# A GRU with expert-choice routing: w_ih by columns on two queues, six pairs of steps multiplied in the head, block products a quad further ahead, and an expert pair's sums in two PSUM banks

## The chip, the cores and the metric

The kernel runs on one core of one Trainium2 chip. The metric is the device time of one execution in microseconds. The program has five engines with queues of their own: TensorE (PE in the profile, with its weight loads as PEld), VectorE (DVE), ScalarE (ACT), GpSimd (POOL) and SyncE (SP, which only issues transfers here). All data is float32, apart from zeros for clearing sums and the counts of the bit search.

## The reference, cut to what matters

```python
gi = x @ W_ih + b_ih;  gh = h @ W_hh + b_hh         # x: 16 x 256 x 512, h: 16 x 512
r = sigmoid(i_r + h_r);  z = sigmoid(i_z + h_z)
n = tanh(i_n + r * h_n)
h = (1 - z) * n + z * h                             # 256 steps, one after the other
S = softmax(states @ router_w + router_b)           # 4096 tokens x 16 experts
G, idx = top_k(S.T, 256)                            # each expert takes its 256 best tokens
out = x + scatter_add(idx, G * (states[idx] @ expert_w + expert_b))
```

All experts share one matrix `expert_w` (512 x 512), so a token's output is its input plus the sum of its gates (G of the experts that took it) times one product of its state. The kernel computes that product for all tokens and multiplies by the gate at the end.

## The kernel before

**Head (lines 430 to 765).** The weights w_ih (3 MB, four row blocks k of 768 KB) and w_hh (3 MB, three gates of 1 MB) and the first two groups of x are loaded on the queues of SP and ScalarE. A group is 8 steps of 16 rows. A pair is two steps. The x-part of the gates (x @ W_ih) of the first four pairs is computed directly: `x_part` (L608) adds one row block k of one pair into a PSUM bank out of the list `held`, k by k as the blocks arrive, and `x_done` (L623) copies the bank with the bias into `ring`, which holds the x-parts of AHEAD = 6 pairs. Meanwhile `mixes` (L635) subtracts column blocks of w_ih from each other on VectorE, for the fast block products of the loop. `keep_clock` fills TensorE's idle time with matmuls of zeros.

**Loop (from L777).** One step s multiplies the state `hs` by w_hh (`h_part`, recorded at L700: 48 matmuls of 32 columns of the array, 96 records), first for r and n, then for z. While ScalarE and VectorE then compute r, tanh, the transposes and the new hs, TensorE is given other work of about the same length, the fill of a step:

- `x_product` (L656, records at L673): the x-parts of later steps, a quad (four steps, two pairs) at a time. A quad's 2 x 2 block product is made of seven block products instead of eight, spread over four steps, with sums kept in `x_bank0`, `x_bank1` and part of `l_bank`. `quad = s // 4 + 2` is the one under work.
- the router's logits of finished groups (in steps marked `apart`), and products of finished states by `expert_w` for the groups 0 to 9 (`expert`, L581), with a bank of `ps_m` per group. `expert_done` copies a finished half out.
- in the last two steps the first pair products of the tail (`expert_for`).

The order on the engines is written out by hand: within `manual_schedule` every engine takes its instructions in the order of the text. VectorE's side work of a step stands after its chain: `x_sums` and `turn_x` (transposing x for the next groups, loaded as `xa` by SP eight steps ahead), `less_max` (maximum for the softmax), `make` (sums of state blocks for pair products) and `mix` (differences of blocks of `expert_w`). They are bound to the position c of a step in its group of eight.

**Tail.** The groups 10 to 27 are taken as nine pairs. For a pair `expert_product` (L284, records at L304) makes seven block products with five sums a to e, each half a PSUM bank wide; ScalarE presets a and e with the bias (`preset_a` L186, `preset_e` L189), copies b from a, c from b, d from b (`copy_of`, L193), and drains finished sums (`drain`, L203 for e, L208); VectorE adds e to the sums of the right halves (L217, or L212 straight from the bank once the gate is known). The order of a pair is

```python
for n, of in ((1, i + 1), (3, i), (7, i), (5, i + 1), (4, i), (2, i + 1), (6, i + 1)):
    yield from expert_product(n, of)
```

so the products of two pairs alternate, and each copy has another pair's product beside it. A yield is half a product's k; `expert_for(n)` runs n units, where a unit is four matmuls of 128 columns. The last four groups are multiplied directly (`late_part`, L111, records at L115). Three banks serve a pair:

```python
pool_of = [(ps_m, "pe"), (ps_m, "pe"), (ps_x, "x0"), (ps_x, "x1"), None, None]
which, half = {"a": (0, lo), "d": (0, hi), "b": (1, lo), "c": (2, lo), "e": (2, hi)}[name]
```

The two entries None are banks of `ps_e`, a pool that is opened only after the loop; until then `catch_up`, which does the copies of finished products, stops at those that need it.

Between the last step and the gate lie the softmax, the transposes of the probabilities and `by_bits` (L1008): a search of 15 bits for each expert's 256th largest probability, one count over all tokens per bit, with seven units of pair products beside each bit. After the gate (L1126, made at L1050) the remaining units run in a loop over `parts`. A counter `owed` rises by 9 with each part, and at 20 a finished group is multiplied by the gate, added to x (`add_gated`, L1056) and stored. At part CHECK = 48 the threshold is counted once more.

Of the kernel before, what the change touches and what calls it, by code (L numbers as in the profile page):

```python
# [17 lines left out]
def kernel(  # L18
# [18 lines left out]
    P = 128  # L37
# [90 lines left out]
    pairs = [(g, g + 1) for g in range(N_EARLY, NG - 4, 2)]  # L128
    pool_of = [(ps_m, "pe"), (ps_m, "pe"), (ps_x, "x0"), (ps_x, "x1"), None, None]
    gated = []  # L130

    def new_bank(i, which):
        pool, tag = pool_of[3 * (i % 2) + which]
        return pool.tile([P, D], F32, name="pe" if tag == "pe" else tag, tag=tag)

# [9 lines left out]
    made += [set_of(room[:, 8 * HD + 4 * HD * i :]) for i in range(N_SETS)]  # L145
    parted = [room[:, 8 * HD + 4 * HD * N_SETS + HD * i :][:, 0:HD] for i in range(2)]
    eb_d = room[:, 10 * HD + 4 * HD * N_SETS :][:, 0:HD]

# [32 lines left out]
    def region(i, name):  # L181
        which, half = {"a": (0, lo), "d": (0, hi), "b": (1, lo), "c": (2, lo), "e": (2, hi)}[name]
        return bank_of(i, which)[:, half]
# [52 lines left out]
    def end_of(i):  # L236
        drain(i, "db")
        if i + 2 < len(pairs):
            preset_a(i + 2)
            preset_e(i + 2)  # L240
        else:
            first = 3 * (i + 2 - len(pairs))
            later.extend((i, n, item) for n, item in enumerate(last_items[first : first + 3]))
            preset_last()

    later = []

    def preset_last():
        i, n, (g, cols) = later.pop(0)
        pe = new_bank(i, n)  # L250
        nc.scalar.copy(pe[:, cols], eb[:, cols])
        last_sums[g, cols.start] = pe
# [23 lines left out]
    def catch_up():  # L276
        while todo:
            n, i = todo[0]
            if pool_of[3 * (i % 2) + 1] is None and n in (1, 5, 6, 7):
                break  # L280
            del todo[0]
            after(n, i)
# [49 lines left out]
    def late_parts():  # L332
# [15 lines left out]
        for item in range(1, len(last_items)):  # L348
            if later:
                preset_last()  # L350
            yield from last_product(item)
# [9 lines left out]
    with (  # L361
# [77 lines left out]
        with tc.manual_schedule(engines={ET.SP, ET.Activation, ET.Pool}):  # L439
            def load_gate(gate, queue, ks=slice(0, KC)):  # L440
                queue.dma_start(
                    out=whh[:, ks, gate, :],
                    in_=w_hh[:, gate * D : (gate + 1) * D].rearrange("(c p) n -> p c n", c=KC)[:, ks, :],
                )

            def load_k(k, queue):
                queue.dma_start(
                    out=wih[:, k].rearrange("p g d -> p (g d)"),
                    in_=w_ih.rearrange("(p c) n -> p c n", c=KC)[:, k, :],
                )  # L450

            nc.gpsimd.dma_start(out=c0, in_=cond)
            nc.sync.dma_start(out=xs[:, 0, :], in_=x[:, 0:TG, :])
            load_k(0, nc.scalar)
            load_k(1, nc.scalar)
            load_k(2, nc.sync)
            load_k(3, nc.sync)
            load_gate(0, nc.scalar)
            nc.sync.dma_start(out=xs[:, 1, :], in_=x[:, TG : 2 * TG, :])
            load_gate(2, nc.sync)  # L460
            load_gate(1, nc.scalar, slice(0, KC - 1))
            load_gate(1, nc.sync, slice(KC - 1, KC))
            nc.scalar.activation(dummy, ones[0:1, 0:1], AF.Sigmoid)
            for dst, src in (
                (b_raw[0:1], b_ih.rearrange("(o g d) -> o g d", o=1, d=D)),
                (b_raw[1:2], b_hh.rearrange("(o g d) -> o g d", o=1, d=D)),
                (b_n, b_hh[2 * D :].rearrange("(o d) -> o d", o=1)),
            ):
                nc.gpsimd.dma_start(out=dst, in_=src)
# [164 lines left out]

        def mixes(part):  # L635
# [4 lines left out]
            nc.vector.tensor_tensor(dst, one, other, ALU.subtract)  # L640

# [75 lines left out]
        with tc.manual_schedule(engines={ET.PE, ET.Activation, ET.DVE, ET.Pool}):  # L717
# [3 lines left out]
            keep_clock(8)  # L721
            held = (r_bank, n_bank, z_bank, x_bank0, x_bank1)

# [12 lines left out]
            for k in range(KC):  # L736
                for p in range(KC):
                    x_part(p, k, held[p], start=False)
                if k == 1:
                    mixes(0)  # L740
                elif k == 2:
                    mixes(1)
                    mixes(3)
                elif k == 3:
                    mixes(2)
                if k == 1:
                    for c in range(KC):
                        nc.tensor.transpose(
                            idles[1][:, B * c : B * (c + 1)], c0[:, P * c : P * (c + 1)], ident[0:B, 0:B]
                        )  # L750
                    nc.vector.tensor_copy(
                        hs[:, :, 0, :], idles[1][:, 0 : KC * B].rearrange("p (k b) -> p k b", b=B)
                    )
                elif k == 2:
                    biases(l_bank)
                    nc.vector.tensor_copy(bias, l_bank.rearrange("p (g d) -> p g d", d=P))
                    nc.scalar.copy(a_sum, bias_f[:, 0:C2])
                    nc.vector.tensor_tensor(spare, bias_f[:, C2 : 2 * C2], bias_f[:, 0:C2], ALU.subtract)
            for p in range(KC):
                x_done(p, held[p])  # L760
                if p == 0:
                    preset_first(0)
                elif p == 2:
                    preset_rest(0)
            spread_x(1, idles[0])
            keep_clock(HEAD_FILL)

        first, second = range(KC // 2), range(KC // 2, KC)

        with tc.manual_schedule(engines={ET.PE, ET.Activation, ET.DVE, ET.Pool, ET.SP}):  # L770
# [6 lines left out]
            for s in range(T):  # L777
# [5 lines left out]
                h_part(s, "z", range(KC))  # L783
                q4, quad = s % 4, s // 4 + 2

# [8 lines left out]

                late_four = q4 == 0 and 2 < quad <= NQ
                if late_four:
# [28 lines left out]
                if s == T - 1:  # L825
                    logits(lgt, range(KC), range(NG - 1, NG), slice(0, TG - 1))
                if s >= T - 2:
                    expert_for((6, 2)[s - T + 2])

# [84 lines left out]
                if apart and c == 6:  # L914
                    less_max(g // KC - 1, lgt)
                if done and s > 6 * TG and (c in (1, 2, 4) or quad >= NQ):
                    g_, half = done.pop(0)
                    expert_done(g_, half)
                    copied += half
                elif s > (N_EARLY + 11) * TG and while_x and c in (1, 2, 4):  # L920
                    make(*while_x.pop(0))

                if c == 0 and g < NG - 1:
                    x_sums(g + 1)
                elif c in (5, 6) and g + 2 < NG:
                    turn_x(g + 2, xa_next, slice(2 * (c - 5), 2 * (c - 4)))

                if c >= KC:
                    if 5 < g < N_EARLY:
                        load_x(g, c - KC, s)  # L930
                elif g + 2 < NG:
                    if c == 0:
                        xa_next = new_xa()
                    nc.gpsimd.tensor_copy(xa_next[quadrant(c), 0, 0:1], hs[quadrant(c), 0, slot(s), 0:1])
                    load_xa(g + 2, xa_next, c, (nc.sync, nc.sync))
                if s > T - TG:
# [46 lines left out]
    with (  # L983
# [5 lines left out]
    ):  # L989
        pool_of[4] = pool_of[5] = (ps_e, "pe")  # L990
# [4 lines left out]
        parted += [rt.tile([P, HD], F32, name=f"part{i}") for i in range(len(pairs) - 2)]  # L995
        by_row = lambda ap: ap.rearrange("p (q b t) -> p b q t", q=QG, b=B)
# [77 lines left out]
        with tc.manual_schedule(engines={ET.PE, ET.Activation, ET.DVE}):  # L1074
# [5 lines left out]
            ps_last = ps_n.tile([P, P], F32, name="ps_last", tag="n")  # L1080
            preset_e(1)
            lg_f = lg.rearrange("p e g -> p (e g)")
# [44 lines left out]

            gated += [add_gated, send]
            owed = 20
# [115 lines left out]
```

## Time and profile before

| | us |
|---|---|
| median of 3 runs | 1117.0 |
| lowest and highest | 1116.86, 1117.44 |
| the profiled execution | 1116.54 |
| its span, first to last instruction | 1114.5 |
| TensorE busy | 1103.0 (99%) |
| VectorE busy | 800.8 (72%) |
| ScalarE busy | 578.7 (52%) |
| gates of step 0 start | 21.00 |
| gates of step 1 start | 26.43 |
| pair products after the gate start | 1073.90 |
| last matmul ends | 1109.56 |

The span is the time from the first instruction to the last; the time of an execution has some 2 us more around it. The profile gives each engine's busy time in the span. A chain of waits follows back from the last instruction what released it; groups of instructions are named by line, engine and tile, with the number of records behind an x. A matmul in float32 leaves two records.

### The profile page before, as it was taken

The page shows a single profiled execution, that of the slowest core. Times are in us where ns is not written, and L with a number is a line of the kernel's source. Part 1 is how long each engine was busy: PE and PEld are TensorE (multiplying, and loading weights), DVE is VectorE, ACT ScalarE, POOL GpSimd, SP SyncE. Part 2 cuts the span into 40 slices and gives each one's busy share as a digit, 9 for nine tenths or more (in the row PEclk, how much of TensorE's full clock was granted, in tenths as well). Part 3 has the DMA queues.
Part 4 walks back from the last instruction along what each step waited for, and adds up shares of the span by engine and source line. Part 5 has one row for each costly group of instructions (what it writes and reads, how often), then busy time and mean ns, then how long its engine had stood idle before and what let it go on. Part 6 is the DMA issues. An engine that isn't in the chain of part 4 may idle for free.

```text
span 1114.5 us, 77084 instructions
## 1 busy us (share of the span) xinstructions
PE 1103.0 (99%) x34242; PEld 956.1 (86%) x34242; DVE 800.8 (72%) x4663; ACT 578.7 (52%) x2648; POOL 31.0 (3%) x176
## 2 busy tenths in 40 slices
PE   8999999999999999999999999999999999999998
PEld 4888888888888888888888888888888888888663
DVE  5666676776767777766767777777777777767885
ACT  1455555555555555555555555555555555554541
POOL 1000000000000000000000000000000000000000
PEclk9999999999999999999999999999999999999999
DMA  7200000000000000000000000000000000003346
GB/s 251 61 13 14 14 14 14 11 21 21 21 21 16 14 14 12 11 12 12 14 14 14 14 12 11 12 12 14 15 14 14 13 12 12 10 5 99 112 144 205
DMA packets 34370, 37.33 MB, mean 33 GB/s; under 512 B 6112, under 2 KB 23776, under 8 KB 34032
## 3 DMA queue, kind: packets, MB, share of 16 engines
q1 hardware_dynamic: 32688, 28.90, 9.0%
q8 instruction: 269, 4.41, 1.7%
q10 hardware_dynamic: 1216, 3.41, 0.9%
q14 instruction: 69, 0.57, 0.2%
q0 software_dynamic: 128, 0.05, 0.0%
HBM read 23.94 MB, written 8.39 MB: 29 GB/s over the span
## 4 chain that ended last, share of the span: by engine, by line
PE 92%; DVE 4%; DMA 2%; ACT 1%; issue 1%; SPq 0%; ACTq 0%; DVEq 0%
PE gates L700 59%; PE x L673 21%; PE gates L673 4%; PE pe L581 3%; PE pe L304 3%; DMA whh<-in_L_cond_W_hh_dram 2%; PE x L304 1%; PE pe L115 1%; DVE nT L882 1%; DVE t L844 1%; DVE zT L885 1%; ACT r L787 1%; ACT t L848 1%; DVE v L893 0%; PE x L115 0%
## 5 line engine op out<-in xcount | busy, mean ns | idle before, releaser
L700 PE MATMUL gates<-whh,hs 128*16 128x128 f32 x24576 | 722.7, 273 | 4.1 <-DVE hs L896 2.3
L700 PEld LDWEIGHTS gates<-whh,hs 128*16 128x16 f32 x24576 | 652.0, 103 | 59.1 <-DVE hs L896 51.5
L787 ACT ACTIVATE r<-gates 128x128 f32<-128x128 f32 x256 | 71.1, 278 | 231.2 <-PE gates L700 231.2
L791 DVE COPY seen<-r 1x1 f32<-1x1 f32 x256 | 36.0, 141 | 201.4 <-ACT r L787 201.3
L885 DVE STREAM_TRANSPOSE zT<-zs 128x32 f32<-128x32 f32 (+1 forms) x768 | 165.8, 216 | 0.7 <-ACT zs L850 0.7
L848 ACT ACTIVATE t<-t 128x64 f32<-128x64 f32 x512 | 103.1, 248 | 103.7 <-DVE t L846 103.7
L882 DVE STREAM_TRANSPOSE nT<-t 128x64 f32<-128x64 f32 x512 | 100.3, 234 | 48.0 <-ACT t L848 48.0
L893 DVE TENSOR_TENSOR v<-u,zT 128x32 f32<-128x32 f32 x512 | 98.7, 193 | 8.8
L673 PE MATMUL x<-wih,xt 128*32 128x192 f32 (+1 forms) x2000 | 103.6, 325 | 0.0
L896 DVE TENSOR_TENSOR hs<-v,nT 128x32 f32<-128x32 f32 x512 | 95.5, 187 | 8.7
L673 PE MATMUL x<-wih,xs 128*32 128x192 f32 x1984 | 92.0, 326 | 0.0
L846 DVE TENSOR_TENSOR t<-t,xs 128x64 f32<-128x64 f32 x512 | 90.7, 219 | 0.0
L844 DVE TENSOR_TENSOR t<-r,gates 128x64 f32<-128x64 f32 x512 | 90.1, 217 | 0.0
L850 ACT ACTIVATE zs<-gates 128x64 f32<-128x64 f32 x512 | 86.8, 221 | 0.8 <-PE gates L700 0.8
L888 DVE TENSOR_TENSOR u<-hs,nT 128x32 f32<-128x32 f32 x512 | 78.4, 153 | 0.0
L673 PEld LDWEIGHTS x<-wih,xt 128*32 128x32 f32 x2000 | 63.6, 110 | 12.0
L673 PEld LDWEIGHTS x<-wih,xs 128*32 128x32 f32 x1984 | 63.2, 110 | 12.1
L506 ACT COPY ht<-hs 128x128 f32<-128x128 f32 (+1 forms) x128 | 51.9, 407 | 0.7 <-DVE hs L896 0.7
L673 PE MATMUL x<-xs 128*32 128x192 f32 (+1 forms) x1056 | 51.7, 316 | 0.0
L673 PE MATMUL x<-xs,xt 128*32 128x192 f32 x992 | 51.7, 326 | 0.0
L673 PE MATMUL gates<-xs 128*32 128x192 f32 x992 | 51.7, 326 | 0.0
L866 ACT COPY x<-x 128x192 f32<-128x192 f32 x62 | 18.8, 303 | 63.0 <-PE x L673 63.0
(200 smaller groups left out, 931.6 us busy)
## 6 DMA issues: line engine op xcount, KB each, us to landing
out_dram<-xs SPq DMA_DIRECT2D x31, 256.0 KB, 3.0
xa<-in_x_dram SPq DMA_DIRECT2D x240, 32.0 KB, 3.0
xs<-in_x_dram SPq DMA_DIRECT2D x28, 256.0 KB, 4.0
wih<-in_L_cond_W_ih_dram ACTq DMA_DIRECT2D x2, 768.0 KB, 6.9
wih<-in_L_cond_W_ih_dram SPq DMA_DIRECT2D x2, 768.0 KB, 10.6
whh<-in_L_cond_W_hh_dram ACTq DMA_DIRECT2D x1, 1024.0 KB, 16.6
whh<-in_L_cond_W_hh_dram SPq DMA_DIRECT2D x1, 1024.0 KB, 18.6
ewr<-in_L_ffn_expert_w_dram SPq DMA_DIRECT2D x4, 256.0 KB, 3.2
```

What stands on the lines that cost most here:

```text
L673: nc.tensor.matmul(dst[quadrant(j), at:to], lhs[:, QD * k : QD * (k + 1)], columns(rows[k], j)[:, at // QD : to // QD], start=False, stop= ...
L700: nc.tensor.matmul(dst[quadrant(j, m)], lhs, columns(whh[:, k, gate_, :], j), start=False, stop=(k == KC - 1), tile_position=(0, QD * j), ...
L787: nc.scalar.activation(r, rr[p % 2], AF.Sigmoid)
L844: nc.vector.tensor_tensor(t[half], r[:, cols], hn[p % 2][:, cols], ALU.mult)
L846: nc.vector.tensor_tensor(t[half], t[half], ring[:, p % AHEAD, 2, cols], ALU.add)
L848: nc.scalar.activation(t[half], t[half], AF.Tanh)
L850: nc.scalar.activation(zs[half], zz[p % 2][:, cols], AF.Sigmoid)
L882: nc.vector.transpose(nT[half], t[half])
L885: nc.vector.transpose(zT[half][:, part], zs[half][:, part])
L888: nc.vector.tensor_tensor(u[half], hs[:, halves[half][2], slot(s), :], of_step(nT[half], odd), ALU.subtract)
L893: nc.vector.tensor_tensor(v[half], u[half], of_step(zT[half], odd), ALU.mult)
L896: nc.vector.tensor_tensor(hs[:, halves[half][2], slot(s + 1), :], v[half], of_step(nT[half], odd), ALU.add)
```

## The change

1. **Head.** Each row block of w_ih is split by columns over the two queues (1024 and 512 columns of the 1536, or 768 and 768). Each gate of w_hh is split in halves by row blocks, in the order r, n, z. The third group's x (`xa`) is loaded in the head. Six pairs instead of four are multiplied directly: four as before, then the second group's x is transposed, and after the row blocks the pairs 4 and 5 follow. The fourth `mixes` goes in halves to steps 0 and 1.
2. **Loop.** The quad under work is `s // 4 + 3`, so the block products end four steps earlier. `x_sums`, `turn_x` and the loads of `xa` move by four steps and one group, and `expert_done` and `make` go to other positions c. The last steps get six units per step for the early groups, and from step 249 on pair products of the tail. `mix` begins at step 244, `preset_a` and `preset_e` at step 248.
3. **Two banks.** A pair's five sums take two banks: a and d share a half, one after the other, e has the other half; b and c share the second bank. The two banks of `ps_e` go to the last groups.
4. **Stores.** `owed` rises by 11 per part, and CHECK is 36.

```diff
-    pool_of = [(ps_m, "pe"), (ps_m, "pe"), (ps_x, "x0"), (ps_x, "x1"), None, None]
+    pool_of = [(ps_x, "x0"), (ps_x, "x1"), (ps_m, "pe"), (ps_m, "pe")]
...
-        which, half = {"a": (0, lo), "d": (0, hi), "b": (1, lo), "c": (2, lo), "e": (2, hi)}[name]
+        which, half = {"a": (0, lo), "d": (0, lo), "e": (0, hi), "b": (1, lo), "c": (1, hi)}[name]
...
-            if pool_of[3 * (i % 2) + 1] is None and n in (1, 5, 6, 7):
-                break
...
-            load_k(0, nc.scalar)
-            load_k(1, nc.scalar)
-            load_k(2, nc.sync)
-            load_k(3, nc.sync)
-            load_gate(0, nc.scalar)
-            nc.sync.dma_start(out=xs[:, 1, :], in_=x[:, TG : 2 * TG, :])
-            load_gate(2, nc.sync)
-            load_gate(1, nc.scalar, slice(0, KC - 1))
-            load_gate(1, nc.sync, slice(KC - 1, KC))
+            for k, at in enumerate((third_k, half_k, half_k, third_k)):
+                load_k(k, nc.scalar, slice(0, at))
+                if k == KC - 1:
+                    nc.sync.dma_start(out=xs[:, 1, :], in_=x[:, TG : 2 * TG, :])
+                load_k(k, nc.sync, slice(at, 3 * D))
+            for gate in (0, 2, 1):
+                for queue, ks in ((nc.scalar, slice(0, KC // 2)), (nc.sync, slice(KC // 2, KC))):
+                    load_gate(gate, queue, ks)
+            xa_next = new_xa()
+            for c in range(KC):
+                load_xa(2, xa_next, c, (nc.sync, nc.sync))
...
-            held = (r_bank, n_bank, z_bank, x_bank0, x_bank1)
+            held = (r_bank, n_bank, z_bank, x_bank0, x_bank1, idles[1])
...
-                elif k == 2:
-                    mixes(1)
-                    mixes(3)
-                elif k == 3:
-                    mixes(2)
...
+                    spread_x(1, idles[0])
+                    x_sums(1)
+                elif k == 3:
+                    mixes(1)
...
-            spread_x(1, idles[0])
-            keep_clock(HEAD_FILL)
+            for p in (KC, KC + 1):
+                for k in range(KC):
+                    for gates in (slice(0, 1), slice(1, 3)):
+                        x_part(p, k, held[p], gates, start=False)
+                if p == KC:
+                    mixes(3)
+                x_done(p, held[p])
+                if p == KC:
+                    nc.scalar.copy(a_sum, bias_f[:, 0:C2])
+            keep_clock(HEAD_FILL, (idles[0],))
...
-                q4, quad = s % 4, s // 4 + 2
+                q4, quad = s % 4, s // 4 + AHEAD // 2
...
-                if s >= T - 2:
-                    expert_for((6, 2)[s - T + 2])
+                if s >= T - TG:
+                    owed = (6, 2, 6, 2)[c - KC] if c >= KC else n
+                    for some in (2, 1, 1, 2) if owed == 6 else (owed,):
+                        expert_for(some)
...
-                if done and s > 6 * TG and (c in (1, 2, 4) or quad >= NQ):
-                    g_, half = done.pop(0)
-                    expert_done(g_, half)
-                    copied += half
-                elif s > (N_EARLY + 11) * TG and while_x and c in (1, 2, 4):
+                if done and s > 6 * TG and (c in (0, 5, 6) or quad >= NQ):
+                    for g_, half in done[: 1 + (quad >= NQ)]:
+                        expert_done(g_, half)
+                        copied += half
+                    del done[: 1 + (quad >= NQ)]
+                elif s > (N_EARLY + 11) * TG and while_x and c in (0, 5, 6):
                     make(*while_x.pop(0))
-                if c == 0 and g < NG - 1:
-                    x_sums(g + 1)
-                elif c in (5, 6) and g + 2 < NG:
-                    turn_x(g + 2, xa_next, slice(2 * (c - 5), 2 * (c - 4)))
+                if s < 2:
+                    mixes(2, slice(s, s + 1))
+                if c == KC and g + 2 < NG:
+                    x_sums(g + 2)
+                elif c in (1, 2) and g + 2 < NG:
+                    turn_x(g + 2, xa_next, slice(2 * (c - 1), 2 * c))
...
-                if s == T - 8:
+                if s == T - 12:
                     nc.vector.tensor_tensor(eb_d, eb[:, hi], eb[:, lo], ALU.subtract)
-                if T - 8 <= s < T - 4:
-                    mix(s - (T - 8))
-                for _ in range((2, 2, 1, 1)[s - T + 4] if s >= T - 4 else 0):
+                if T - 12 <= s < T - 8:
+                    mix(s - (T - 12))
+                if s >= T - TG:
                     make(*ahead.pop(0))
-                if s == T - 4:
+                if s == T - TG:
                     preset_a(0)
                     preset_e(0)
-                if s == T - 2:
+                elif s > T - TG:
                     catch_up()
+                if s == T - 5:
                     preset_a(1)
+                    preset_e(1)
...
-        NTOP, CHECK = 8, 48
+        NTOP, CHECK = 8, 36
...
-                owed += 9
+                owed += 11
```

More of the change, by code (lines that the diff above doesn't have):

```diff
@@ L128 @@
     pairs = [(g, g + 1) for g in range(N_EARLY, NG - 4, 2)]
-    pool_of = [(ps_m, "pe"), (ps_m, "pe"), (ps_x, "x0"), (ps_x, "x1"), None, None]
+    pool_of = [(ps_x, "x0"), (ps_x, "x1"), (ps_m, "pe"), (ps_m, "pe")]
     gated = []
     def new_bank(i, which):
-        pool, tag = pool_of[3 * (i % 2) + which]
-        return pool.tile([P, D], F32, name="pe" if tag == "pe" else tag, tag=tag)
+        pool, tag = pool_of[2 * (i % 2) + which]
+        return pool.tile([P, D], F32, name=tag, tag=tag)
     room = wih.rearrange("p k g d -> p (k g d)")
@@ L146 @@
     parted = [room[:, 8 * HD + 4 * HD * N_SETS + HD * i :][:, 0:HD] for i in range(2)]
+    parted.append(room[:, 11 * HD + 4 * HD * N_SETS :][:, 0:HD])
     eb_d = room[:, 10 * HD + 4 * HD * N_SETS :][:, 0:HD]
@@ L241, in end_of @@
         else:
-            first = 3 * (i + 2 - len(pairs))
-            later.extend((i, n, item) for n, item in enumerate(last_items[first : first + 3]))
-            preset_last()
+            rest = last_items[2:4] if i + 2 == len(pairs) else last_items[4:]
+            later.extend((lambda n=n: new_bank(i, n), item) for n, item in enumerate(rest))
     later = []
     def preset_last():
-        i, n, (g, cols) = later.pop(0)
-        pe = new_bank(i, n)
+        bank, (g, cols) = later.pop(0)
+        pe = bank()
         nc.scalar.copy(pe[:, cols], eb[:, cols])
@@ L348, in late_parts @@
         for item in range(1, len(last_items)):
-            if later:
+            while later:
                 preset_last()
@@ L444, in load_gate, with load_k @@
                 )
-            def load_k(k, queue):
+            def load_k(k, queue, cols):
                 queue.dma_start(
-                    out=wih[:, k].rearrange("p g d -> p (g d)"),
-                    in_=w_ih.rearrange("(p c) n -> p c n", c=KC)[:, k, :],
+                    out=wih[:, k].rearrange("p g d -> p (g d)")[:, cols],
+                    in_=w_ih.rearrange("(p c) n -> p c n", c=KC)[:, k, cols],
                 )
+            half_k, third_k = 3 * D // 2, 2 * D
             nc.gpsimd.dma_start(out=c0, in_=cond)
             nc.sync.dma_start(out=xs[:, 0, :], in_=x[:, 0:TG, :])
-            load_k(0, nc.scalar)
-            load_k(1, nc.scalar)
-            load_k(2, nc.sync)
-            load_k(3, nc.sync)
-            load_gate(0, nc.scalar)
-            nc.sync.dma_start(out=xs[:, 1, :], in_=x[:, TG : 2 * TG, :])
-            load_gate(2, nc.sync)
-            load_gate(1, nc.scalar, slice(0, KC - 1))
-            load_gate(1, nc.sync, slice(KC - 1, KC))
+            for k, at in enumerate((third_k, half_k, half_k, third_k)):
[9 more added lines that the diff above has]
+                load_xa(2, xa_next, c, (nc.sync, nc.sync))
             nc.scalar.activation(dummy, ones[0:1, 0:1], AF.Sigmoid)
@@ L633, with mixes @@
         e_sum = l_bank[:, P : P + C2]
-        def mixes(part):
+        def mixes(part, ks=slice(0, 2)):
             half = lambda h, cols: wih[:, 2 * h : 2 * h + 2].rearrange("p k g d -> p k (g d)")[:, :, cols]
@@ L639, in mixes @@
             dst, one, other = ((t1, b12, b11), (t2, b22, t1), (b12, b22, b12), (nt4, b21, t2))[part]
-            nc.vector.tensor_tensor(dst, one, other, ALU.subtract)
+            nc.vector.tensor_tensor(dst[:, ks], one[:, ks], other[:, ks], ALU.subtract)
         def x_sums(g):
@@ L740 @@
                     mixes(0)
-                elif k == 2:
-                    mixes(1)
-                    mixes(3)
-                elif k == 3:
-                    mixes(2)
-                if k == 1:
                     for c in range(KC):
                         nc.tensor.transpose(
-                            idles[1][:, B * c : B * (c + 1)], c0[:, P * c : P * (c + 1)], ident[0:B, 0:B]
+                            idles[0][:, B * c : B * (c + 1)], c0[:, P * c : P * (c + 1)], ident[0:B, 0:B]
                         )
                     nc.vector.tensor_copy(
-                        hs[:, :, 0, :], idles[1][:, 0 : KC * B].rearrange("p (k b) -> p k b", b=B)
+                        hs[:, :, 0, :], idles[0][:, 0 : KC * B].rearrange("p (k b) -> p k b", b=B)
                     )
@@ L756 @@
                     nc.vector.tensor_copy(bias, l_bank.rearrange("p (g d) -> p g d", d=P))
-                    nc.scalar.copy(a_sum, bias_f[:, 0:C2])
                     nc.vector.tensor_tensor(spare, bias_f[:, C2 : 2 * C2], bias_f[:, 0:C2], ALU.subtract)
+                    spread_x(1, idles[0])
+                    x_sums(1)
+                elif k == 3:
+                    mixes(1)
             for p in range(KC):
@@ L793 @@
                     nc.scalar.copy((x_bank0 if q4 > 1 else x_bank1)[0:1, D - 1 : D], r[0:1, 0:1])
-                late_four = q4 == 0 and 2 < quad <= NQ
+                late_four = q4 == 0 and AHEAD // 2 < quad <= NQ
                 if late_four:
@@ L915 @@
                     less_max(g // KC - 1, lgt)
-                if done and s > 6 * TG and (c in (1, 2, 4) or quad >= NQ):
-                    g_, half = done.pop(0)
-                    expert_done(g_, half)
-                    copied += half
-                elif s > (N_EARLY + 11) * TG and while_x and c in (1, 2, 4):
-                    make(*while_x.pop(0))
-                if c == 0 and g < NG - 1:
-                    x_sums(g + 1)
-                elif c in (5, 6) and g + 2 < NG:
-                    turn_x(g + 2, xa_next, slice(2 * (c - 5), 2 * (c - 4)))
-                if c >= KC:
+                if done and s > 6 * TG and (c in (0, 5, 6) or quad >= NQ):
[4 more added lines that the diff above has]
+                elif s > (N_EARLY + 11) * TG and while_x and c in (0, 5, 6):
+                    make(*while_x.pop(0))
+                if s < 2:
[4 more added lines that the diff above has]
+                    turn_x(g + 2, xa_next, slice(2 * (c - 1), 2 * c))
+                if c < KC:
                     if 5 < g < N_EARLY:
-                        load_x(g, c - KC, s)
-                elif g + 2 < NG:
-                    if c == 0:
+                        load_x(g, c, s)
+                elif g + 3 < NG:
+                    if c == KC:
                         xa_next = new_xa()
-                    nc.gpsimd.tensor_copy(xa_next[quadrant(c), 0, 0:1], hs[quadrant(c), 0, slot(s), 0:1])
-                    load_xa(g + 2, xa_next, c, (nc.sync, nc.sync))
+                    nc.gpsimd.tensor_copy(xa_next[quadrant(c - KC), 0, 0:1], hs[quadrant(c - KC), 0, slot(s), 0:1])
+                    load_xa(g + 3, xa_next, c - KC, (nc.sync, nc.sync))
                 if s > T - TG:
@@ L989 @@
     ):
-        pool_of[4] = pool_of[5] = (ps_e, "pe")
         sT = rt.tile([P, QG * P], F32, name="sT")
@@ L994 @@
         made.append(set_of(rt.tile([P, 4 * HD], F32, name="made")))
-        parted += [rt.tile([P, HD], F32, name=f"part{i}") for i in range(len(pairs) - 2)]
+        parted += [rt.tile([P, HD], F32, name=f"part{i}") for i in range(len(pairs) - 3)]
         by_row = lambda ap: ap.rearrange("p (q b t) -> p b q t", q=QG, b=B)
@@ L1080 @@
             ps_last = ps_n.tile([P, P], F32, name="ps_last", tag="n")
-            preset_e(1)
             lg_f = lg.rearrange("p e g -> p (e g)")
@@ L1128 @@
             gated += [add_gated, send]
+            later.extend((lambda: ps_e.tile([P, D], F32, name="pe", tag="pe"), item) for item in last_items[:2])
+            preset_last()
+            preset_last()
             owed = 20
```

## The prediction

> **What bounds the kernel now.** I read the profile page first, then the chain of waits over a few steps of the loop, the busy time of each engine by stage, the timeline of TensorE in the head, and the waits of the tail. The page:
>
> ```profile
> span 1114.5 us, 77084 instructions
> PE 1103.0 (99%) x34242; PEld 956.1 (86%) x34242; DVE 800.8 (72%) x4663; ACT 578.7 (52%) x2648; POOL 31.0 (3%) x176
> PE 92%; DVE 4%; DMA 2%; ACT 1%; issue 1%; SPq 0%; ACTq 0%; DVEq 0%
> ```
>
> TensorE is busy 99% of the span and 92% of the chain. That alone would say that any product taken away is time won, so I looked at where a product ends a wait. The chain over three loop steps, and four stages (start:end | length, busy us of each engine, granted clock, DMA share, GB/s):
>
> ```profile
> 402.96 2.65 PE gates L700 x96
> 405.61 1.30 PE x L673 x32
> 406.91 2.67 PE gates L700 x96
> ...
> 6.50:20.40 13.90, 13.84 (x174) 6.10 (x174) 9.23 (x12) 1.12 (x3) 0.18 (x1) 1.00 1.03 375
> 20.40:26.43 6.03, 4.72 (x133) 3.47 (x132) 4.34 (x22) 2.85 (x14) 0.00 (x0) 1.00 0.15 46
> 1044.80:1067.30 22.50, 22.26 (x514) 14.97 (x510) 19.40 (x71) 11.97 (x37) 0.00 (x0) 1.00 0.26 77
> 1073.70:1109.60 35.90, 35.80 (x566) 18.14 (x558) 26.31 (x47) 11.38 (x31) 0.00 (x0) 1.00 0.74 228
> ```
>
> A loop step is 2.66 us of gate products and 1.30 us of block products, 3.96 us in all. The chain from hs through the gates, tanh, the transposes and back to hs also measures 3.96 us (gates of step 253 start 1025.45, the next 1029.41, with less fill between), so the loop has two equal limits and is not shortened by removing fill. In the head (first row) TensorE is busy 13.84 of 13.90 us: what is added there is paid. So it is behind the gate (last row, 35.80 of 35.90): what is removed there is won. The granted clock is 1.00 in each stage.
>
> **Head.** Two pairs more are multiplied by x_part before step 0: 2 pairs x 4 k. One (pair, k) costs 0.65 us: the timeline has four of them in 10.35-12.95 us.
>
> ```profile
> 10.35 2.14 PE L613 MATMUL gates<-wih,xt 128*32 128x384 f32 x24
> 12.31 0.83 PE L613 MATMUL x<-wih,xt 128*32 128x384 f32 x8
> ...
> 21.00 0.63 PE L700 MATMUL gates<-whh,hs 128*16 128x128 f32 x16 [0.39 <-ACT gates L596]
> 22.15 1.69 PE L700 MATMUL gates<-whh,hs 128*16 128x128 f32 x50 [0.51 <-DMA whh<-in_L_cond_W_hh_dram]
> ...
> 26.43 0.84 PE L700 MATMUL gates<-whh,hs 128*32 128x128 f32 x21 [0.41 <-DVE hs L896]
> ```
>
> TensorE's sum until step 0: four k-passes 4 x 2.60 = 10.4, c0's transposes 0.47, biases 1.14, x1's transposes 0.75, the two new pairs 8 x 0.65 = 5.2, clock filling 0.45; together 18.4 us. They started at 7.66 before, with k0 wholly on ScalarE's queue. Now SP carries a third of k0 behind x's first 256 KB, and the first product can wait for it: 7.7 to 8.3, I take 7.9 (x landed at 6.45; 256 KB at the 390 GB/s of this stage is 0.7 us, of which the queues' sharing hides part). Step 0 then starts at 26.3. W_hh's last piece landed at 22.9 and only changes order, so step 0 no longer waits for it and takes 3.96 instead of 5.43 us (21.00 to 26.43). Step 1 starts at 30.26 against 26.43: **+3.8 us**. Half of the product time is paid by what step 0 waited before. Bounds: +3.2 (start 7.3, k0 in two halves arriving early) and +4.5 (start 8.3, and 0.2 for step 0's split fill).
>
> SP now issues 4 pieces of w_ih, 3 of W_hh and 8 loads of 32 KB for xa where it issued 2 and 2; at the 0.57-0.61 us of an issue in the chain the last leaves SP some 10 us in. Only xa stands behind (256 KB more, 0.7 us of the stream), and it is first read in step 1. DVE's six mixing steps (four of 1.76 us, one moved into steps 0 and 1 by halves) and x_done (0.47 each) end at about 27.3 of the 28.4 at which step 0's block product reads the mixed weights: 1.1 us cover; without it the difference enters the path once.
>
> The Trainium skill, "DMA: Bandwidth & Descriptors", section "Issuing engines are not separate DMA queues", states that transfers started from several engines run on the same 16 engines and interleave, so that a second queue saves only issue time. It speaks against the split by columns as a gain in bytes; by it k0 would land no earlier, and the sum keeps its start of 7.9. The rows of this case gave that start already: both queues together moved 375 GB/s at a DMA share of 1.03.
>
> **Loop.** The quad of block products is gone at its end: from step 244 on, expert units of 4 matmuls x 128 columns fill the steps. Turns of x are moved off the steps that also hold less_max (1.05 us on VectorE): seven such steps last 4.03-4.06 instead of 3.96, which comes to -0.5. Against it: in steps 249-255, without block products, the gates wait for two semaphores (hs from VectorE, the bank from ScalarE) and the period is 4.03-4.09, some 0.085 more; after the change that holds for steps 245-255, four more, +0.34. Step 244 has 1.70 us of VectorE extras where about 1.54 fit: +0.17. The loads of xa behind SP's and POOL's queues only move by four steps. Sum **0.0**, bounds -0.5 and +0.5.
>
> **Tail.** Before, the pair products do 8 units in the loop, 144 up to the gate, 164 behind it. Now 30 units lie in steps 249-255 (2, 6, 6, 6, 2, 6, 2), where they take the room that the missing quad leaves and the chain covers them; 144 stay ahead of the gate, so 142 are left behind it. The chain of the tail has 16 records of pair products in 0.86 us, which are four units: 0.216 each. 22 x 0.216 = **-4.75 us**, at full price since TensorE is the limit there; 31.1 us of it then remain. VectorE has 26.3 us of work in those 31.1, and the stores are paced at 11 of 20 instead of 9, so they follow. The stores' bytes stay, so DMA's share goes from 0.74 to about 0.86, still below one. The last product to the end (1109.56 to the span's end) stays 4.9.
>
> The bit search ahead of it: 15 bits in 24.2 us; three bits took 1.82 us instead of 1.55 since VectorE's add waits for ScalarE's copy.
>
> ```profile
> DVE ht L217 <- ACT ht L208: 1.2, 3, 0.4
> ...
> PEld pe L304 <- ACT pe L193: 1.4, 2, 0.8
> ```
>
> The products are 22 units ahead now, and these sums are copied earlier: **-0.5**, between -0.8 (all three vanish) and +0.3 (softmax's exponent stands behind five copies on ScalarE instead of three).
>
> **Two banks.** d now takes a's half of the bank and e the other half, so a pair's later copy needs the earlier one drained. The program's order stays: a is drained after product 2, and d is copied after product 7, with the next pair's product 5 (0.86 us) between copy and use; copy and drain take 0.30 + 0.36. The trace doesn't show the new sharing. Bounds: 0, and a stall like the second row above (1.4 over 2, so 0.7) at each of 8 pairs, 5.6 us. I take 0, since 0.86 covers 0.66.
>
> The Trainium skill's "PSUM — Partial Sum Buffer", section "PSUM bank collisions raise a hardware error", asks that engines be kept apart by bank and 32-partition quadrant, whatever the columns. By it products into one half would also wait for copies from the other, and the sum would move toward its upper end; no row of before shows a pair packed in this way.
>
> **Sum.** The profiled execution took 1116.54 us (span 1114.5): 1116.54 + 3.8 + 0.0 - 4.75 - 0.5 + 0 = 1115.1. The median of the runs, 1117.0, lies 0.46 above that execution, so I forecast **1115.6 us**.
>
> **Rivals.** (1) The head is free: the two pairs hide under W_hh's arrival, as step 0 waited there. Then step 0 is late by only 0 to 0.5 and the time is 1115.6 - 3.5 = 1112. For it: the 0.51 and the fill between 21.0 and 24.3 us. Against it: 13.84 busy of 13.90 in front, and of the 5.2 us only 1.4 fits into step 0's excess. (2) Slower: the two banks. If ScalarE, which also writes the last groups' presets, gets to d's copy over 0.2 us late (0.86 - 0.66), every pair stalls, and 0.7 x 8 = 5.6 gives 1121.2. For it: the two stalls of that kind that three banks already had. Against it: ScalarE is busy 11.4 of 35.9 us there. (3) The removal of units does not reach the end, because VectorE or the stores set it: then -4.75 shrinks to about -2, 1118.3, inside the bound of no change. For it: 26.3 of 31.1 and a DMA share of 0.86; against it: VectorE's last stores already wait for TensorE (0.89 and 1.33 us).
>
> **How the numbers follow.** Two tenths of a per cent, about what a measurement of this kernel can tell from no change, is 2.23 us: faster means below 1114.8, slower above 1119.2. The forecast's case has 0.70; its known bounds (head -0.6 and +0.7, loop 0.5 each way, bits -0.3 and +0.8) reach 1114.2 to 1117.6 if all go one way, and unknown ones can widen that, so I give it 0.19 below 1114.8, 0.50 within and 0.01 above. Rival 1 has 0.11 (faster), rival 2 0.11 (slower), rival 3 0.08 (same). That makes 0.30 faster, 0.58 same, 0.12 slower. The range 1113.0 to 1118.8 takes in rival 3 and the upper part of rival 1's, and leaves out about 0.1 at each end.
>
> **What would show it.** In the changed trace step 1 starts at 30.0 to 30.7 with no wait for W_hh; steps keep 3.96; from the gate to the last product 31 us remain, with TensorE over 99% busy; the bits take 23.7. The prediction is wrong if step 1 starts before 29.5, if ScalarE's copies appear as releasers of TensorE in each pair, or if the stretch behind the gate stays above 32.5 us.

## The result and the profile after

| | before | after |
|---|---|---|
| median, us | 1116.9 (4 runs) | 1123.9 (4 runs) |
| lowest to highest | 1116.63 to 1117.44 | 1123.73 to 1124.03 |
| span of the profiled execution | 1114.5 | 1121.9 |

The change makes the kernel slower: the ratio is 1.0062, with a 95% interval of 1.0045 to 1.0079. The forecast was 1115.6.

First the page of the changed kernel: its span, the engines' busy time, and the chain by engine.

```profile
span 1121.9 us, 77177 instructions
PE 1104.7 (98%) x34290; PEld 957.1 (85%) x34290; DVE 802.4 (72%) x4664; ACT 577.0 (51%) x2637; POOL 30.1 (3%) x172
PE 93%; DVE 4%; ACT 1%; DMA 1%; issue 0%; SPq 0%; DVEq 0%; ACTq 0%
```

TensorE's work grew by 1.7 us and the span by 7.4. So 5.7 us more are idle on the engine that was the limit. The busy time by stage shows where (start:end | length, busy us per engine, clock, DMA share, GB/s): the time up to the first product, the rest of the head, the bit search, and the stretch behind the gate.

```profile
6.50:9.29 2.79, 1.16 (x6) 0.70 (x7) 0.89 (x4) 0.00 (x0) 0.00 (x0) 1.00 1.04 381
9.29:27.80 18.51, 18.51 (x298) 9.86 (x299) 10.85 (x20) 2.62 (x6) 0.00 (x0) 1.00 0.76 257
1051.99:1078.41 26.42, 24.78 (x565) 15.50 (x555) 22.00 (x76) 13.31 (x39) 0.00 (x0) 1.00 0.27 74
1082.20:1117.10 34.90, 32.00 (x482) 15.17 (x482) 25.71 (x46) 9.54 (x26) 0.00 (x0) 1.00 0.76 235
```

TensorE is idle 1.6 of 2.8 us before the first product, 1.6 us in the bit search (0.2 before, in 22.5 us of it), and 2.9 us behind the gate (0.1 before). TensorE's timeline tells for whom it waits; the bracket at a line's end is the idle time ahead of it and its releaser.

```profile
9.29 2.14 PE L614 MATMUL gates<-wih,xt 128*32 128x384 f32 x24 [1.61 <-DMA wih<-in_L_cond_W_ih_dram]
...
31.75 2.83 PE L701 MATMUL gates<-whh,hs 128*32 128x128 f32 x96 [0.48 <-DVE hs L904]
...
1056.66 1.05 PE L302 MATMUL x<-ewr,xs 128*32 128x256 f32 x16
1058.25 0.86 PE L302 MATMUL x<-wih,xs 128*32 128x256 f32 x16 [0.55 <-ACT ht L209]
...
1088.11 1.07 PE L302 MATMUL x<-wih 128*32 128x256 f32 x16 [1.48 <-DVE ht L213]
...
1095.17 1.07 PE L302 MATMUL pe<-wih 128*32 128x256 f32 x16 [0.81 <-DVE ht L213]
```

The drains that end two of these waits, on ScalarE and on VectorE:

```profile
1057.83 0.37 ACT L209 COPY ht<-x 128x256 f32<-128x256 f32 x1 [0.54 <-PE x L302]
...
1085.65 2.07 DVE L1068 SCALAR_TENSOR_TENSOR xs<-ht,gate,xs 128x512 f32<-128x512 f32 x3
1087.63 0.42 DVE L213 TENSOR_TENSOR ht<-x,part 128x256 f32<-128x256 f32 x1
```

The line at 1056.66 is product 3, which completes c. The line at 1058.25 is product 7 of the same pair, which writes b. L209 is ScalarE's copy that drains a finished sum, here c, and L213 is VectorE's add that does the same once the gate is known. Product 7 doesn't read c. But b and c now are the two halves of one bank, and product 7 follows product 3 at once. Three bits have this wait; they last 2.30 us where the others last 1.55. Behind the gate VectorE is the one that drains c. For the waits of 1.48 and 0.81 us its add comes after the multiplications by the gate that belong to the stores (L1068, 0.75 us for one): the add at 1087.63 begins 1.0 us after product 3 has ended. For the third wait (0.62 us, at 1102.03) VectorE was idle for 0.38 us before its add, so that one is the add alone, without a store ahead of it.

A second pair of halves meets in the same way, once: at 1046.73, ahead of the first count, product 2 is held for 0.46 us while it writes a, and ScalarE's drain of e (L204), the other half of that bank, ends the wait.

Following the same marks through both traces (r, ScalarE's first instruction of a step, then the first count, the end of the bits, the last sums of the gate and the last matmul) gives the whole difference; the last column is what the prediction had for the stretch:

| stretch | before | after | difference | forecast |
|---|---|---|---|---|
| start to r of step 1 | 28.01 | 33.34 | +5.33 | +3.8 |
| steps 1 to 244 | 962.82 | 962.29 | -0.53 | -0.5 |
| steps 244 to 255 | 44.30 | 45.88 | +1.58 | +0.5 |
| to the first count | 9.70 | 10.48 | +0.78 | 0 |
| bit search | 24.97 | 26.41 | +1.44 | -0.5 |
| to the gate | 3.52 | 3.77 | +0.25 | 0 |
| behind the gate | 36.16 | 34.94 | -1.22 | -4.75 |
| last matmul to the end | 5.03 | 4.75 | -0.28 | 0 |
| sum | | | +7.35 | -1.45 |

### The profile page after: what moved, and what is told of

It reads as the page before. It is cut to its first block, busy times and chain, and to the rows that moved or that the text cites. A ratio compares the mean times of both kernels' runs of the same rounds, so it can differ in the third digit from the quotient of the medians.

```text
span 1121.9 us, 77177 instructions
## 1 busy us (share of the span) xinstructions
PE 1104.7 (98%) x34290; PEld 957.1 (85%) x34290; DVE 802.4 (72%) x4664; ACT 577.0 (51%) x2637; POOL 30.1 (3%) x172
## 4 chain that ended last, share of the span: by engine, by line
PE 93%; DVE 4%; ACT 1%; DMA 1%; issue 0%; SPq 0%; DVEq 0%; ACTq 0%
PE gates L701 59%; PE x L674 20%; PE gates L674 3%; PE pe L582 3%; PE x L302 3%; PE pe L302 2%; PE pe L115 1%; DVE nT L890 1%; PE gates L614 1%; DMA wih<-in_L_cond_W_ih_dram 1%; DVE t L852 1%; DVE xs L1068 1%; DVE zT L893 1%; ACT r L793 1%; ACT t L856 0%
## 5 line engine op out<-in xcount | busy, mean ns | idle before, releaser
L674 PE MATMUL x<-wih,xt 128*32 128x192 f32 (+2 forms) x1968 | 101.7, 325 | 0.0
L874 ACT COPY x<-x 128x192 f32<-128x192 f32 x61 | 18.5, 303 | 62.0 <-PE x L674 62.0
```

Source lines behind the costliest of these rows:

```text
L674: nc.tensor.matmul(dst[quadrant(j), at:to], lhs[:, QD * k : QD * (k + 1)], columns(rows[k], j)[:, at // QD : to // QD], start=False, stop= ...
```

## The experiments

Two theories stood at first. **Theory 1, shared bank:** c's drain and product 7 meet in one bank, and this is where the gain of the tail goes. **Theory 2, VectorE late:** the new pace of stores keeps VectorE from draining in time. Beside them stood a cause of its own for the head: the first row block of w_ih, split over two queues, lands late. Times are compared with runs of the kernel before on the same chip: 1116.4 us for the runs "c beside a", "product 5 between 3 and 7", "first row block on one queue" and "the kernel before with w_ih split", and 1116.2 for the other four.

**c beside a.** The pair's sums are put into the same two banks in another way.

```diff
-{"a": (0, lo), "d": (0, lo), "e": (0, hi), "b": (1, lo), "c": (1, hi)}
+{"a": (0, lo), "d": (0, lo), "c": (0, hi), "b": (1, lo), "e": (1, hi)}
```

> The changed kernel with c and e exchanged: a, d and c lie in one bank, b and e in the other. Theory 1 (shared bank): in the changed kernel product 7 writes b while the copy that drains c out of the same bank is still under way, once per pair. Then three bits of the search fall from 2.30 us to 1.55 to 1.82 (1.5 us), the stalls behind the gate of 1.48, 0.81 and 0.62 us go (2.9), and two ahead of the first count of about 0.5 shrink: together 4.5 to 5, so 1119 to 1119.5 us. Theory 2 (VectorE is late behind the gate because stores come at 11 of 20 and its adds stand behind them): the bits fall as well, but the waits behind the gate only move to the next product that needs a drained half; 1122 us.

Measured: 1116.5 us, ratio to before 1.0001 (0.9991 to 1.0010). That is 6.8 us less than the change, measured by the distance of each to before (0.15 and 7.0). All 15 bits take 1.55 us. The stages of the bit search and behind the gate in this kernel, and the same two products:

```profile
1050.90:1075.06 24.16, 24.16 (x557) 16.41 (x556) 22.23 (x77) 13.00 (x39) 0.00 (x0) 1.00 0.28 80
1078.60:1110.40 31.80, 31.60 (x482) 15.39 (x482) 25.44 (x46) 9.38 (x26) 0.00 (x0) 1.00 0.81 257
```

```profile
1055.57 1.05 PE L302 MATMUL x<-ewr,xs 128*32 128x256 f32 x16
1056.43 0.84 PE L302 MATMUL x<-wih,xs 128*32 128x256 f32 x16
```

TensorE waits nowhere in the bits and once, for 0.19 us, behind the gate, with the same products, the same work on VectorE and the same pace of stores. Only the sharing of banks is different. Now two other products lie between 3 and the next one that writes into c's bank. Theory 2 is out as the main cause: of its 1122 nothing is seen, and the waits behind the gate have not moved on. The gain is larger than the 4.5 to 5 expected. From r of step 255 to the end it is 6.7 us by the traces: 1.2 up to the first count, 2.25 in the bits, 0.25 to the gate, 3.1 behind it, and 0.1 lost at the end. The 1.2 includes the wait of product 2 for e's drain, since a and e no longer share a bank.

**Product 5 between 3 and 7.** In the changed kernel the order of products is changed.

```diff
-for n, of in ((1, i + 1), (3, i), (7, i), (5, i + 1), (4, i), (2, i + 1), (6, i + 1)):
+for n, of in ((1, i + 1), (3, i), (5, i + 1), (7, i), (4, i), (2, i + 1), (6, i + 1)):
```

> The changed kernel with the next pair's product 5 moved from behind product 7 to in front of it. Theory 1 (shared bank): product 5 covers the drain of c, so the waits in front of product 7 go, but now nothing covers the copy of d in front of product 4 (0.30 and 0.36 us): a wait of about 0.6 us per pair stands there, released by ScalarE's copy, and behind the gate the adds of VectorE no longer release TensorE. 1122 to 1123.5 us. Theory 2 (VectorE late): the waits behind the gate stay with VectorE as their releaser, and the copy of d comes on top; 1126 us.

Measured: 1122.3 us, ratio 1.0053 (1.0036 to 1.0070). In this order the first pair's d is copied from b only after product 4, so that one block product drops out of its sum; the amount of work is the same. TensorE's timeline where it waits:

```profile
1059.74 0.63 PE L302 MATMUL x<-wih,ht 128*32 128x256 f32 x7 [0.48 <-ACT x L194]
...
1087.44 1.07 PE L302 MATMUL x<-wih 128*32 128x256 f32 x16 [0.61 <-DVE ht L213]
1088.99 1.07 PE L302 MATMUL x<-wih,ht 128*32 128x256 f32 x16 [0.48 <-ACT x L194]
```

In the bits product 7 no longer waits: one foreign product (0.86 us) covers the drain. The wait is now in front of product 4, and its releaser is the copy of d (L194), which product 4 needs itself, as it adds into d; product 5 covered that copy before. There are not enough foreign products in this order to cover both. Behind the gate two waits on VectorE's add are left (0.61 and 0.62), against the expectation that all would go. At the first, the add stands behind stores and begins 1.0 us after product 3, which one product covers only in part. The second is the last pair's, whose products 3 and 7 follow each other in lines of their own that this edit leaves as they were.

**Stores at 10 of 20.** In the changed kernel `owed += 11` becomes `owed += 10`.

> The changed kernel, unrepaired, with stores at 10 of 20 a part in place of 11. Theory 1 (shared bank): the waits behind the gate (1.48, 0.81, 0.62 us) stand since product 7 waits for an add of VectorE out of c's bank, which stands behind one or two stores of 0.75 us; a slower pace takes some stores out of the way, the waits shrink by at most a third, 1123 us. Theory 2 (VectorE is too slow for the pace): the waits shrink to a few tenths, 1121.5 us. The bits of 2.30 us stay in both.

Measured: 1124.8 us, ratio 1.0073 (1.0058 to 1.0088), slower than both expected; 8.6 above before, where the change was 7.0 above. The waits behind the gate are 1.48, 0.62 and 0.62 us in place of 1.48, 0.81 and 0.62, about as theory 1 had it. What neither theory had is the end: from the last matmul 6.9 us instead of 4.8. At this pace VectorE still multiplies two finished groups (at 1113.75) shortly before the last sums (1116.54), and SP issues the last five stores within 3.5 us. Part of the 2.1 us may be chance, as the same stretch lasts 4.8 to 5.9 us in the other profiles at a pace of 11. So the pace of 11 was not the fault, and 10 is no gain; in the repaired kernel 10 was not tried.

**First row block on one queue.** In the changed kernel the first block of w_ih goes whole to ScalarE's queue, the others stay split.

```diff
-                load_k(k, nc.scalar, slice(0, at))
+                load_k(k, nc.scalar, slice(0, at) if k else slice(0, 3 * D))
...
-                load_k(k, nc.sync, slice(at, 3 * D))
+                if k:
+                    load_k(k, nc.sync, slice(at, 3 * D))
```

> The changed kernel with the first row block of w_ih whole on ScalarE's queue, as before the change; the other three stay split. If the third of it behind x on SP's queue made the first product late (9.29 instead of 7.66 us), the first product returns to 7.7 and step 1 from 31.75 to about 30.2: 1.5 us less, 1122.4 us. If the stream as a whole sets the head, the later row blocks are then waited for, and the time stays 1123.9 us.

Measured: 1122.15 us, ratio 1.0052 (1.0035 to 1.0069); 5.8 above before, where the change was 7.0 above. TensorE's timeline:

```profile
7.74 2.14 PE L615 MATMUL gates<-wih,xt 128*32 128x384 f32 x24
...
30.21 2.83 PE L702 MATMUL gates<-whh,hs 128*32 128x128 f32 x96 [0.48 <-DVE hs L905]
```

The first product starts at 7.74 and step 1 at 30.21; 1.55 us less in the trace, and 1.2 less by the times. The later blocks arrive in time as before, so it was one piece, not the stream, that was late. Heads of one program text differ between profiles: with the whole block the first product starts at 7.74 to 8.48 in four kernels, with the split one at 9.18 to 9.60 in four others. The means are 1.3 us apart.

**The kernel before with w_ih split.** Four pairs, w_hh as before; only the columns of w_ih are divided.

> The kernel before with only the columns of w_ih split over both queues (1024 and 512, or 768 and 768), four pairs in the head, w_hh as before. If the split delays the first row block by 1.6 us, the first product starts at 9.3, but some 1.05 us of that lies in the time in which step 0 waited for w_hh and was filled: step 1 at 27.0 instead of 26.43, 1117.6 us. If w_hh alone sets step 1, 1117.0; if w_hh is delayed as well, 1118.5.

Measured: 1117.5 us, 1.1 above before, ratio 1.0009 (1.0000 to 1.0019). The first product starts at 9.25 and step 1 at 27.39 in place of 26.43, which is +0.96 where 0.6 was expected. The direction is as expected. The time is hardly clear of noise (the interval begins at 1.0000), and less than the 1.6 us of the first product reaches step 1, since step 0 waits for w_hh anyway.

**Both repairs.**

> The changed kernel with both repairs: c beside a (and e beside b), and the first row block of w_ih whole on ScalarE's queue. If the two causes are separate, their gains add: the first alone came to the level of the kernel before (1116.5 against 1116.4), the second alone took 1.75 off the changed kernel. So 1114.8 us, 1.6 below the kernel before, which is about what the prediction's sum gave. If the earlier head runs into another wait, 1116 us.

Measured: 1115.4 us, 0.8 below before, ratio 0.9992 (0.9983 to 1.0001), so not clear of no difference, and 0.6 above what was expected. By the distances to before, the two repairs alone are worth 6.8 and 1.2 us; together that would be 1.1 below. In this profile step 1 begins 0.36 us later than with the first block's repair alone, which is within the spread of heads given above, and no cause is claimed. Behind the gate the stretch is 31.8 us.

**Wide units in the late steps.** The kernel with both repairs; in the late steps six units are issued as three times 256 columns.

```diff
-                    for some in (2, 1, 1, 2) if owed == 6 else (owed,):
+                    for some in (2, 2, 2) if owed == 6 else (owed,):
```

> As the kernel with both repairs, but the six units of a late step are issued as three times two (256 columns each) in place of 2, 1, 1, 2. Steps 249 to 255 last 4.1 to 4.35 us, where 4.05 was forecast. If the narrow matmuls stretch the fill (1.41 us in place of 1.30 in the steps with six pair units), steps 250, 251 and 255 lose about 0.1 each, 0.3 to 0.5 us in all. If the stretch is in the gates themselves, the same time within 0.2 us.

Measured: 1114.75 us, ratio 0.9986 (0.9977 to 0.9995). This version beats both kernels: 1.4 us below before. From r of step 244 to r of step 255 it takes 45.0 us in place of 45.8, but not where expected: the periods that end at r of 253 and 254 fall from 4.34 and 4.28 to 4.05 and 4.03, and the one that ends at 250 stays at 4.27. Of the 0.29 of the first, some 0.10 is in the six units themselves (1.39 and 1.29 us on the chain) and 0.17 in the gates behind them (2.92 and 2.75). Why the gates take longer there, and why the period ending at 254 falls, though its two units are issued as before, stays open.

**No pair products in the late steps.** The kernel with both repairs; pair products only in the last two steps, as before.

> As the kernel with both repairs, but pair products of the tail run only in the last two steps, as before the change; the other 22 units move behind the gate. Behind the gate TensorE is the limit, so 22 x 0.216 = 4.75 us are added there. If pair products with their copies are what stretches steps 249 to 253, these steps return to 4.05 (0.9 us less): 1114.8 + 3.9 = 1118.7 us. If the stretch is that of any late step without block products, 1119.5 us.

Measured: 1120.5 us, ratio 1.0036 (1.0023 to 1.0050); 5.1 above the kernel with both repairs, where 3.9 or 4.7 were expected. Behind the gate 36.4 us against 31.8: +4.6 for 22 units, which is the 4.75 of the prediction. The periods ending at 250 to 254 return to 4.03 to 4.08, and the stretch from 244 to 255 loses 1.1 us. So pair products with their copies do stretch those steps, the one ending at 250 too, which the wide units left as it was; the one ending at 249 stays at 4.18, for which no run shows the cause. Of what lies above the expectation, 0.9 us is in the bits, 25.1 against 24.2 us: with fewer products ahead, three bits take 1.81 again.

## Why the prediction was wrong, by its steps

**Two banks, the step that failed.** I took 0 for the sharing, since I looked at one pair of sums only, a and d, for which product 5 of the next pair covers copy and drain. I did not ask the same of the second bank. There c is complete after product 3, product 7 is the next on TensorE, and it writes b in the same bank. No foreign product lies between. The diff showed it in one line, and the order of products stood next to it. Exchanging c and e is worth 6.7 us by the traces, which is most of the 8.8 us between the forecast's -1.45 and the measured +7.35. The second rival had the mechanism's kind, the number of stalls and nearly the price (0.7 x 8 = 5.6, 1121.2), but its condition was wrong: not ScalarE 0.2 us late at d's copy, but a cover that is absent by the order itself. With that it should have been the likeliest case.

The Trainium skill's "PSUM — Partial Sum Buffer", section "PSUM bank collisions raise a hardware error", asks for a guard by bank and quadrant and not by address. As to addresses, that is what the trace shows of this program: product 7 writes columns 0 to 255 and waits 0.55 us for a copy that reads columns 256 to 511. A bank is one tile of the program here, so these runs do not tell whether the wait is set for the bank or for the tile. I had quoted the rule as one that moves the sum to its upper end, and then kept 0. No run here shows what would happen without the wait; it was not tried.

Two of the signs named ahead came true in the trace: ScalarE's copies release TensorE in the bits, and the stretch behind the gate is 34.9 us, above 32.5.

**Head, mis-sized.** The sum on TensorE was right: 18.4 us forecast, 18.5 measured (9.29 to 27.80), and the step behind it 3.95. The start was wrong: 9.29, where I took 7.9 and gave 8.3 as the latest. I added 256 KB behind x at the full rate, less a part. In the trace x landed at 6.4 us and the piece at 9.16. From 6.50 to 9.29 the queues moved 1.06 MB, 0.44 on SP's queue and 0.60 on ScalarE's, and the piece is only 0.26 MB: at least three quarters of what passed behind x were other pieces. Why this piece got no larger share is not shown. The price of the split was not the 0.24 us that I took (7.66 to 7.9) but 1.6 in these two profiles, and 1.3 between the means of four heads each. With the block on one queue, step 1 starts at 30.21, against 30.26 forecast; that this is so close is partly luck, since the same head gives 30.38 to 30.94 in three other profiles.

The Trainium skill's rule in "DMA: Bandwidth & Descriptors", section "Issuing engines are not separate DMA queues", that a second queue brings no bytes, is not contradicted: with the blocks split the stage from 6.50 to 9.29 moved 381 GB/s, and 382 before. No run here uses one queue only.

**Loop, partly right.** -0.53 over steps 1 to 244 is the forecast of the turns of x. Steps 245 to 248 cost 0.08 each, as the two waits were priced; no run separates the waits from the missing block products. Mis-sized were steps 249 to 255, 1.25 us in all where none was added: the pair products put into them, narrow and with copies in between. The run without pair products gives back 1.1 us of it and the run with wide units 0.7.

**Units moved ahead of the gate, right.** The term -4.75 was hidden by the bank's waits. With the sharing repaired, the stretch behind the gate is 4.3 us shorter than before (31.82 against 36.16), and taking the units out of the loop costs 4.6. **Bits, right once repaired:** -0.8, the bound at which all three waits vanish. The third rival (VectorE or the stores as the limit) is excluded at a pace of 11 by the run with c beside a; at a pace of 10 the stores lengthen the end.

## What to carry to other kernels

When accumulators are packed into fewer banks, list for each bank, in the engine's own order, every reader and the next writer of any of its columns, and count the foreign products in between; one pair of tiles that is covered says nothing of the next. Where a term of a sum is bounded by 0 and 5.6 and its cover is only argued, write the order out before choosing an end. Put a load that the first product needs first on a queue and in one piece: here a third of it, behind 256 KB of another tensor, landed at 9.16 us, and the whole block, first on ScalarE's queue, was there before the first product started at 7.74.

## What the runs showed that was not expected

A drain of 0.42 us became a stall of 1.48 us on another engine, because in the order written for VectorE the add stood behind multiplications of 0.75 us for the stores. A slower pace of stores made that no better, and the end was some 2 us longer. And with six units as 256, 128, 128 and 256 columns, in place of three times 256, a step lasted up to 0.29 us longer although the same columns are multiplied.
